# Products over eight neighbours in place, sums in halves, and one repeating load for each tile of neighbours

## The chip, the cores and the metric

One core of a Trainium2 chip runs the kernel in one launch. The metric is device time in microseconds, the median of three runs. The engines have a queue of instructions each and run side by side: PE (TensorE) multiplies matrices, PEld stands for its weight loads, DVE (VectorE) and ACT (ScalarE) work on rows of 128 partitions, POOL (GpSimd) helps, and SP (SyncE) issues transfers. SPq, DVEq and so on stand for an engine's queue.

## The reference, cut to what matters

The model is three residual blocks on `x` of shape (16, 64, 256). Inputs, weights and the two blocks that the change doesn't touch are left out.

```python
x = x + xattn(layernorm(x), ctx)      # quantised self and cross attention, ctx (16, 1601, 256)
x = x + attn(layernorm(x))            # below
x = x + ffn(layernorm(x))

def attn(x, ...):                     # NH = 16 heads, HD = 16, NB = 8 blocks, bt = 64 // 8 = 8 tokens
    h = rmsnorm(x, attn_norm_w)
    qkv = bitlinear(h, qkv_w).reshape(B, S, 3, NH, HD)
    ...
    q = apply_rope(q, cos, sin)
    k = apply_rope(k, cos, sin)
    qb, kb, vb = (blk(q), blk(k), blk(v))                       # (B, NB, NH, bt, HD)
    scores = jnp.einsum('bnhqd,bnhkd->bnhqk', qb, kb) * HD ** -0.5
    scores = jnp.where(causal, jnp.finfo(scores.dtype).min, scores)
    attn = jax.nn.softmax(scores, axis=-1)
    ctx = jnp.einsum('bnhqk,bnhkd->bnhqd', attn, vb)
    ...
    x1 = x + bitlinear(ctx, o_w)
    hn = rmsnorm(x1, ffn_norm_w)
    gate, val = jnp.split(hn @ ffn_up_w.T, 2, axis=-1)
    return x1 + bitlinear(jax.nn.silu(gate) * val, ffn_down_w)
```

Every token attends to the at most eight tokens of its own block: a row of queries meets eight rows of keys and eight rows of values, its neighbours. `bitlinear` quantises its input by rows (`act_quant`) and has ternary weights.

## The kernel before, in words

**Tiles and streams.** The 1024 rows of `x` are eight tiles of 128 rows, `NT = 8`, sixteen blocks of eight tokens in each. For every tile there are four units of the cross attention (two halves of the heads, two batch items), and a unit walks through the 1601 rows of `ctx` in chunks. A chunk loads context (`ctxT`, L608, and `ctxN`, L617), projects keys (`ps_k`, L624), copies them as 16-bit halves (`kh`, L651), stores these to DRAM (`kd`, L655), loads them back transposed (`kT`, L665, a transposing transfer), multiplies with the queries (`s`, L696), exponentiates on ACT (`P`, L706), keeps a running maximum on DVE (`M`, L715; maxima over the transposed `tr_m`, L721 and L723, then `tr_r`, L438), applies the maximum (`P`, L754 on DVE and L758 on ACT) and sums over the values (`acc`, L772). A unit ends in reciprocals and divisions (`rvx` and `pq`, L785 to L790), transposes (`tr_pc`, L799) and `po_x` (L863), whose result goes through `q_y` (L875) and a rounding to 8 bits into `cat` (L319) and the output projection (`po_p`, L332, weights in two halves `w_hi` and `wproj`, L309 and L310). The self attention (`ps_q`, `ps_kv`, L379, weights `wq` and `wkv`, loaded on L301) runs beside it.

**The stage of the change.** `last_parts(i)` (L1068) computes for tile i the block attention and the feed-forward part. It runs while the units of later tiles are at work; the last tile's has no units left beside it. Normalise and quantise (`act_quant`, whose transposes are `tr_aq`, L997), project to `qk` and `v3`, rotate, and then, for all tiles but the last:

- the rotated keys and the values go to DRAM (`kv`, L1127) in two halves of eight heads, 128 columns each;
- `near(kv, e, a)` (L1003) loads a half back so that each of the 128 rows holds all eight rows of its block, 8 x 128 numbers. Eight transfers do that: number k writes the k-th row of each of the sixteen blocks, 16 rows of 4 KB, 64 KB;
- `product` (L1010), for each half of the keys, multiplies with the row's queries into a new tile `prod` (L1013) and sums over the 16 features (L1014) into the scores `sc`;
- softmax over the eight neighbours (L1139 to L1150);
- `product` again, for each half of the values, multiplies with the scores and sums over the eight neighbours into `cx`;
- `act_quant` of `cx`, the transposes `tr_aq`, the output projection `po_o` (L1168), and the feed-forward part.

The values are loaded (L1138) after the scores' products have been written down. The last tile (7) doesn't use `near` and `product`: it selects neighbours by matmuls (`block_scores`, `block_values`), and its `block_values` sums in halves (L1061 to L1063).

**Buffers.** `near` and `prod` tiles come from the pool `wp`, ten buffers of 128 x 1024 numbers, which the weights (`wq`, `wkv`, `wqx`, `wproj`, `w_hi`, `sel` and others) use as well. A middle tile takes four buffers for `near` and four for `prod`.

**Order.** The streams are generators on a heap: each has a step and a rank, and what it yields, changed by a list of offsets by hand (`PACE`), is the step at which it goes on. This gives the order in which the program is written down. A scheduler then orders each engine's instructions by its own estimates, so the order on an engine can differ from the program's and can move with an edit. On the chip each queue runs in that order and nothing overtakes. SP issues nearly all transfers; eight semaphores for them are used in turn, and an issue waits for the one eight before it. In the last span, groups of the late feed-forward (`late_chunk`, matmuls `pgu_late`, L1255, four to a chunk) are put between the steps of the last tile to keep PE at work.

```python
def paced(name, gen):
    d = PACE.get(name, ())
    for k, w in enumerate(gen):
        yield max(w + (d[k] if k < len(d) else 0), 0.01)
```

Of the kernel before, what the change touches and what calls it, by code (L numbers as in the profile page):

```python
# [14 lines left out]
F32 = mybir.dt.float32  # L15
# [4 lines left out]
ALU = mybir.AluOpType  # L20
AX = mybir.AxisListType
PSUM = bass.MemoryType.PSUM

P = 128
# [49 lines left out]
def body(tc, ctx, a):  # L74
    nc = tc.nc
    V, A, PE, GP = nc.vector, nc.scalar, nc.tensor, nc.gpsimd
# [3 lines left out]
    wp = ctx.enter_context(tc.tile_pool(name="wp", bufs=10))  # L80
# [861 lines left out]
    def b1(name, dt=F32):  # L942
        return one.tile([P, 256 if dt == F32 else 512], dt, tag="b1", name=name, bufs=4)

    def b2(name):
        return one.tile([P, 512], F32, tag="b2", name=name, bufs=3)
# [56 lines left out]
    def near(kv, e, a):  # L1003
        t = wp.tile([P, 1024], F32, tag="w", name="near")
        src = kv[e, a].rearrange("(n j) c -> n (j c)", j=8)
        for k in range(8):
            nc.sync.dma_start(out=t.rearrange("(n t) x -> n t x", t=8)[:, k, :], in_=src)
        return t

    def product(out, x, y, order):  # L1010

        t = wp.tile([P, 1024], F32, tag="w", name="prod")
        V.tensor_tensor(t.rearrange("p (h j d) -> p h j d", h=8, j=8), x, y, ALU.mult)  # L1013
        V.reduce_sum(out, t.rearrange("p (h j d) -> p " + order, h=8, j=8), axis=AX.X)  # L1014

    def gathered(src, c):

# [8 lines left out]
    def block_scores(rotate, r1, r2, sc):  # L1026
        rotate(16, 32, V)
        V.tensor_tensor(r1[:, H : 2 * H], r1[:, H : 2 * H], r2[:, H : 2 * H], ALU.add)
        yield 1
        keys = [gathered(r1[:, H : 2 * H], c) for c in range(4)]  # L1030
        rotate(0, 16, V)
        V.tensor_tensor(r1[:, 0:H], r1[:, 0:H], r2[:, 0:H], ALU.add)
        yield 1
        for d in range(2):
            fill("sc%d" % d)
            t = wp.tile([P, 1024], F32, tag="w", name="prod").rearrange("p (j x) -> p j x", j=4)
            for e in range(2):
                V.tensor_tensor(
                    t[:, 2 * e : 2 * e + 2], keys[2 * d + e], r1[:, 0:H].unsqueeze(1).to_broadcast([P, 2, H]), ALU.mult
                )  # L1040
            V.reduce_sum(
                sc[:, :, 4 * d : 4 * d + 4].rearrange("p h j -> p j h"), t.rearrange("p j (h d) -> p j h d", h=16), axis=AX.X
            )
            yield 1

    def block_values(sc, v3, cx):
        ts = []
        for d in range(2):
            fill("av%d" % d)
            t = wp.tile([P, 1024], F32, tag="w", name="prod").rearrange("p (j x) -> p j x", j=4)  # L1050
            for e in range(2):
                c = 2 * d + e
                V.tensor_tensor(
                    t[:, 2 * e : 2 * e + 2].rearrange("p j (h d) -> p j h d", h=16),
                    gathered(v3, c).rearrange("p j (h d) -> p j h d", h=16),
                    sc[:, :, 2 * c : 2 * c + 2].rearrange("p h j -> p j h").unsqueeze(3).to_broadcast([P, 2, 16, 16]), ALU.mult,
                )
            ts.append(t.rearrange("p j x -> p (j x)"))
            yield 1
        x, y = ts  # L1060
        V.tensor_tensor(x, x, y, ALU.add)  # L1061
        V.tensor_tensor(x[:, 0:512], x[:, 0:512], x[:, 512:1024], ALU.add)
        V.tensor_tensor(cx, x[:, 0:H], x[:, H : 2 * H], ALU.add)  # L1063
        yield 1
# [3 lines left out]
    def last_parts(i, start):  # L1068
# [6 lines left out]
        h = b1("h")  # L1075
# [26 lines left out]
        r1, r2 = b2("r1"), b2("r2")  # L1102
        r24 = r2.rearrange("p (h e d) -> p h e d", h=32, e=2)

        def rotate(h0, h1, eng):
            n = h1 - h0
            eng.tensor_tensor(
                r1.rearrange("p (h d) -> p h d", h=32)[:, h0:h1], qk.rearrange("p (h d) -> p h d", h=32)[:, h0:h1],
                rope[:, 0:16].unsqueeze(1).to_broadcast([P, n, 16]), ALU.mult,
            )  # L1110
            for e in range(2):
                V.tensor_tensor(
                    r24[:, h0:h1, e, :], q4[:, h0:h1, 1 - e, :],
                    rope[:, 16 + 8 * e : 24 + 8 * e].unsqueeze(1).to_broadcast([P, n, 8]), ALU.mult,
                )

        sc = one.tile([P, 16, 8], F32, tag="sc3", name="sc3")
        if last:
            yield from block_scores(rotate, r1, r2, sc)
        else:  # L1120
            rotate(0, 32, GP)
            yield 1
            V.tensor_tensor(r1, r1, r2, ALU.add)
            yield 1
            kv = dram.tile([2, 2, P, P], F32, tag="kv3", name="kv3")
            for e, t in ((0, r1[:, H : 2 * H]), (1, v3)):
                nc.sync.dma_start(out=kv[e].rearrange("a p c -> p a c"), in_=t.rearrange("p (a c) -> p a c", a=2))  # L1127
            yield 1
            near_k = [near(kv, 0, a) for a in range(2)]
            yield 2  # L1130
            for a in range(2):
                product(
                    sc[:, 8 * a : 8 * a + 8, :],
                    r1[:, a * P : (a + 1) * P].rearrange("p (h d) -> p h d", h=8).unsqueeze(2).to_broadcast([P, 8, 8, 16]),
                    near_k[a].rearrange("p (j h d) -> p h j d", j=8, h=8), "h j d",
                )
                yield 1
            near_v = [near(kv, 1, a) for a in range(2)]  # L1138
        V.tensor_tensor(sc, sc, cmask.unsqueeze(1).to_broadcast([P, 16, 8]), ALU.add)  # L1139
# [12 lines left out]
        cx = one.tile([P, H], F32, tag="cx3", name="cx3")  # L1152
        if last:
            yield from block_values(sc, v3, cx)
        else:
            for a in range(2):
                product(
                    cx[:, a * P : (a + 1) * P].rearrange("p (h d) -> p h d", h=8),
                    sc[:, 8 * a : 8 * a + 8, :].unsqueeze(3).to_broadcast([P, 8, 8, 16]),
                    near_v[a].rearrange("p (j h d) -> p h j d", j=8, h=8), "h d j",  # L1160
                )
                yield 1
        to = ternary_piece(1536, 512).rearrange("p (k o) -> p k o", k=2)
        yield 1
# [179 lines left out]
    for i in range(NT):  # L1344
        base = 52 * i
        for hh in range(2):
            for bb in range(2):
                unit(i, hh, bb, base + 26 * hh + 13 * bb)
            spawn(base + 26 * hh + 13 + 34 - 2 + (2, 1)[hh], 6.5, paced("pair", pair_out(i, hh, 4 if i < NT - 1 or hh == 0 else None)))
        ln0, sa0, qx0 = SCHEDULE[i] if i in SCHEDULE else (  # L1350
            base - 22, [base + o for o in (-15, 0, 8, 21)], [base + o for o in (-16, -7, 15, 18)]
        )
        spawn(ln0, 1.0, paced("ln" if i else "ln_first", ln_tile(i)))
        for p in range(4):
            spawn(sa0[p] - 2, 5.0, paced("sa", self_attention(i, p)))
            spawn(qx0[p] - 2, 3.0, paced("qx", queries(i, p)))
        l0 = base + {NT - 3: 95, NT - 2: 88, NT - 1: 82}.get(i, 90)
        spawn(l0, 4.5, paced("last" if i < NT - 1 else "last_tile", last_parts(i, l0)))
    spawn(-4.5, 1, bias_rows())
    spawn(60, 5.7, ternary())  # L1360
    order = [(kind, p) for p in range(4) for kind in ("wq", "wkv", "wqx", "wproj")]
# [76 lines left out]
```

## Time and profile before

| what | value |
|---|---|
| median of 3 runs | 2376.91 us (2375.15, 2376.91, 2381.84) |
| the profiled execution | 2381.09 us |
| its span, first to last instruction | 2379.3 us |
| granted TensorE clock, mean of the span | 0.996 |
| bytes moved, mean rate | 482.82 MB, 203 GB/s |
| costliest groups on PE | `acc` L772 799.8 us, `ps_k` L624 757.7 us, `s` L696 411.9 us |

The table's durations are sums over all instructions of a line. The profile is of one execution; times within it count from its first instruction. A line of the timeline gives start and duration in us, engine, line, operation, the tiles written and read, their shapes and how many instructions stand together; in square brackets is how long the engine was idle before and what ended the wait. A line that groups instructions by form gives their number, the least, median and largest duration in ns, and the first and last start in us.

### The profile page before, as it was taken

The page shows a single profiled execution, that of the slowest core. Times are in us where ns is not written, and L with a number is a line of the kernel's source. Part 1 is how long each engine was busy: PE and PEld are TensorE (multiplying, and loading weights), DVE is VectorE, ACT ScalarE, POOL GpSimd, SP SyncE. Part 2 cuts the span into 40 slices and gives each one's busy share as a digit, 9 for nine tenths or more (in the row PEclk, how much of TensorE's full clock was granted, in tenths as well). Part 3 has the DMA queues.
Part 4 walks back from the last instruction along what each step waited for, and adds up shares of the span by engine and source line. Part 5 has one row for each costly group of instructions (what it writes and reads, how often), then busy time and mean ns, then how long its engine had stood idle before and what let it go on. Part 6 is the DMA issues. An engine that isn't in the chain of part 4 may idle for free.

```text
span 2379.3 us, 40465 instructions
## 1 busy us (share of the span) xinstructions
PE 2318.1 (97%) x12501; PEld 1766.1 (74%) x12509; DVE 1844.9 (78%) x4786; ACT 1670.7 (70%) x3729; POOL 746.6 (31%) x967
## 2 busy tenths in 40 slices
PE   7999999999999999999999999999999999999997
PEld 4677777777787777777778777777777777677876
DVE  6777768878878788787887879777888777876766
ACT  6767767776776777767776777777677777676631
POOL 3323223332332333332332323334333333232200
PEclk9999999999999999999999999999999999999999
DMA  8989878777977698776887769777698776965332
GB/s 271 281 234 252 231 177 240 206 186 187 269 206 195 173 224 246 195 202 176 234 230 196 202 183 248 217 196 190 179 258 212 188 184 173 276 174 140 116 98 72
DMA packets 682094, 482.82 MB, mean 203 GB/s; under 512 B 463932, under 2 KB 591896, under 8 KB 681880
## 3 DMA queue, kind: packets, MB, share of 16 engines
q1 hardware_dynamic: 681592, 480.08, 75.4%
q8 instruction: 100, 1.64, 0.3%
q14 instruction: 114, 0.93, 0.1%
q10 hardware_dynamic: 288, 0.17, 0.0%
HBM read 268.93 MB, written 112.85 MB: 160 GB/s over the span
## 4 chain that ended last, share of the span: by engine, by line
PE 75%; DVE 9%; DMA 5%; ACT 4%; issue 3%; POOL 3%; SPq 0%; ACTq 0%; DVEq 0%; POOLq 0%
PE acc L772 23%; PE ps_k L624 22%; PE s L696 13%; PE po_x L863 2%; PE po_p L332 2%; DMA kd<-kh 2%; PE ps_q L379 2%; ACT P L706 1%; DMA kT<-kd 1%; PE tr_pc L799 1%; POOL rsx L568 1%; DVE P L754 1%; PE sc L490 1%; POOL rs L226 1%; PE po_f L1274 1%
## 5 line engine op out<-in xcount | busy, mean ns | idle before, releaser
L772 PEld LDWEIGHTS acc<-ctxN,P 128*128 128x128 f32 (+1 forms) x4160 | 713.3, 191 | 212.6 <-issue 134.9
L772 PE MATMUL acc<-ctxN,P 128*128 128x257 f32 (+5 forms) x4160 | 799.8, 338 | 5.4 <-DMA ctxN<-in_ctx_n 3.3
L624 PE MATMUL ps_k<-wkx,ctxT 128*128 128x512 f32 x1600 | 757.7, 595 | 11.6 <-DVE wkx L1331 9.4
L567 POOL TENSOR_SCALAR vx<-ss 128x4 f32<-128x4 f32 (+1 forms) x402 | 162.2, 403 | 1215.3 <-DVE ss L564 803.9
L706 ACT ACTIVATE P<-s,rsx 128x128 f32<-128x128 f32 x1536 | 441.0, 374 | 142.4 <-PE s L696 131.4
L568 POOL TENSOR_TENSOR rsx<-vx,nhalf 128x4 f32<-128x4 f32 (+1 forms) x402 | 442.6, 1101 | 32.7
L624 PEld LDWEIGHTS ps_k<-wkx,ctxT 128*128 128x128 f32 x1600 | 277.3, 191 | 208.9 <-issue 188.9
L696 PE MATMUL s<-qx,kT 128*128 128x128 f32 x3072 | 411.9, 277 | 8.2 <-ACT qn L389 4.4
L696 PEld LDWEIGHTS s<-qx,kT 128*128 128x128 f32 x3072 | 377.2, 192 | 24.8 <-ACT qn L389 6.2
L715 DVE TENSOR_TENSOR M<-P,M 128x512 f32<-128x512 f32 (+1 forms) x384 | 263.0, 685 | 167.4 <-ACT P L706 146.0
L758 ACT ACTIVATE P<-P 128x512 f32<-128x512 f32 (+1 forms) x416 | 266.6, 642 | 154.9 <-DVE P L754 153.6
L651 ACT COPY kh<-ps_k 128x1024 uint16<-128x1024 uint16 x360 | 366.8, 1019 | 8.9 <-DMA kd<-kh 8.9
L559 ACT ACTIVATE sq<-ps_k 128x512 f32<-128x512 f32 (+1 forms) x402 | 243.4, 605 | 156.2 <-PE ps_k L624 128.0
L564 DVE TENSOR_REDUCE ss<-sq 128x4 f32<-128x512 f32 (+1 forms) x402 | 272.0, 677 | 18.9 <-ACT sq L559 18.5
L754 DVE TENSOR_TENSOR P<-P,mx 128x512 f32<-128x512 f32 (+1 forms) x416 | 283.2, 681 | 0.0
L226 POOL TENSOR_TENSOR rs<-ve,nhalf 128x4 f32<-128x4 f32 (+2 forms) x112 | 114.9, 1027 | 241.4 <-DVE ve L223 218.6
L232 DVE TENSOR_SCALAR qn<-qn,mv,rs 128x128 f32<-128x128 f32 x256 | 77.2, 340 | 47.8 <-POOL rs L226 47.1
L310 DVE TENSOR_TENSOR wproj<-wproj,w_hi 128x1024 fp32r<-128x1024 f32 x60 | 73.0, 1218 | 12.9 <-ACT w_hi L309 12.2
L309 ACT CAST w_hi<-wproj 128x1024 fp32r<-128x1024 f32 x60 | 63.4, 1058 | 26.8 <-DMA wproj<-wproj 26.0
L219 DVE BATCH_NORM_STATS2 st<-qn 128x6 f32<-128x128 f32 x256 | 64.5, 270 | 18.8 <-ACT qn L389 18.8
L332 PE MATMUL po_p<-wproj,cat 128*128 128x256 f32 x272 | 67.1, 293 | 0.0
L332 PE MATMUL po_p<-w_hi,cat 128*128 128x256 f32 x240 | 65.9, 308 | 0.9 <-ACT qk L1091 0.9
(254 smaller groups left out, 2763.7 us busy)
## 6 DMA issues: line engine op xcount, KB each, us to landing
kd<-kh SPq DMA_DIRECT2D x375, 256.0 KB
ctxT<-in_ctx SPq DMA_DIRECT2D x192, 256.0 KB
ctxN<-in_ctx_n SPq DMA_DIRECT2D x384, 128.0 KB
wproj<-wproj SPq DMA_DIRECT2D x68, 512.0 KB
wq<-wq SPq DMA_DIRECT2D x32, 512.0 KB
wkv<-wkv SPq DMA_DIRECT2D x32, 512.0 KB
wqx<-wqx SPq DMA_DIRECT2D x32, 512.0 KB
near<-kv SPq DMA_DIRECT2D x224, 64.0 KB
```

What stands on the lines that cost most here:

```text
L332: PE.matmul(po[:, 0:H], lhsT=cat[:, h, :], rhs=w[:, h * H : (h + 1) * H], start=h + e == 0, stop=h == 3 and e == len(ws) - 1,)
L559: A.activation(sq[:n], ps[:n], AF.Square)
L564: ordered("dve", V.reduce_sum(ss[:n], sq[:n].rearrange("p (g d) -> p g d", g=4), axis=AX.X))
L568: ordered("pool", GP.tensor_tensor(rs[:n], ve[:n], nhalf[:n, 0:4], ALU.pow))
L624: PE.matmul(ps[:n, :], lhsT=st["cxT"][c // 2][:, k, o : o + n], rhs=wkx[:, k, 512 * hh : 512 * (hh + 1)], start=k == 0, stop=k == 1,)
L651: A.copy(t, src.bitcast(U16).rearrange("p (c e) -> p e c", e=2))
L696: PE.matmul(ps[:n, g * P : (g + 1) * P], lhsT=kT[:, g, 0:n], rhs=qxs[i, hh][:, bb, 2 * g : 2 * g + 2, :].rearrange("p h s -> p (h s)"), st ...
L706: A.activation(pc[:, g * P : (g + 1) * P], ps[:, g * P : (g + 1) * P], AF.Copy, scale=rs[:, g : g + 1])
L715: ordered("dve", V.tensor_tensor(st["M"][:n], pc[:n], st["M"][:n], ALU.max))
L754: ordered("dve", V.tensor_tensor(pc[:n], pc[:n], st["mx"][:n].rearrange("p g q -> p (g q)"), ALU.add))
L758: A.activation(pc[:n], pc[:n], AF.Exp)
L772: m = PE.matmul(ps, lhsT=pc[:n, g * P : (g + 1) * P], rhs=cx[:n, o : o + w], start=g < 3 and c == 0, stop=c == NC - 1, skip_group_check=g ...
```

## The change

Two things are done in the middle tiles 0 to 6, and the last tile's code stays. `near` issues one transfer in place of eight: its source names the block's 4 KB row eight times (a repeat with a step of zero as the second dimension, behind the sixteen blocks), its destination is the whole tile of 128 rows. `product` is replaced by two functions that need no tile of their own. `near_scores` multiplies into the `near` tile itself, laid out neighbour by neighbour, and sums over the features. `near_values` multiplies into the `near` tile, and sums over the neighbours by adding the upper half to the lower: 512 numbers, 256, and 128 into `cx`.

```diff
     def near(kv, e, a):
         t = wp.tile([P, 1024], F32, tag="w", name="near")
         src = kv[e, a].rearrange("(n j) c -> n (j c)", j=8)
-        for k in range(8):
-            nc.sync.dma_start(out=t.rearrange("(n t) x -> n t x", t=8)[:, k, :], in_=src)
+        nc.sync.dma_start(out=t, in_=src.unsqueeze(1).to_broadcast([16, 8, 1024]))
         return t

-    def product(out, x, y, order):
-
-        t = wp.tile([P, 1024], F32, tag="w", name="prod")
-        V.tensor_tensor(t.rearrange("p (h j d) -> p h j d", h=8, j=8), x, y, ALU.mult)
-        V.reduce_sum(out, t.rearrange("p (h j d) -> p " + order, h=8, j=8), axis=AX.X)
+    def near_scores(out, x, y):
+
+        y = y.rearrange("p (j x) -> p j x", j=8)
+        V.tensor_tensor(y, x.unsqueeze(1).to_broadcast([P, 8, P]), y, ALU.mult)
+        V.reduce_sum(out, y.rearrange("p j (h d) -> p h j d", h=8), axis=AX.X)
+
+    def near_values(out, x, y):
+
+        y4 = y.rearrange("p (j h d) -> p j h d", j=8, h=8)
+        V.tensor_tensor(y4, x.rearrange("p h j -> p j h").unsqueeze(3).to_broadcast([P, 8, 8, 16]), y4, ALU.mult)
+        for n in (512, 256):
+            V.tensor_tensor(y[:, 0:n], y[:, 0:n], y[:, n : 2 * n], ALU.add)
+        V.tensor_tensor(out, y[:, 0:P], y[:, P : 2 * P], ALU.add)
...
             near_k = [near(kv, 0, a) for a in range(2)]
             yield 2
             for a in range(2):
-                product(
-                    sc[:, 8 * a : 8 * a + 8, :],
-                    r1[:, a * P : (a + 1) * P].rearrange("p (h d) -> p h d", h=8).unsqueeze(2).to_broadcast([P, 8, 8, 16]),
-                    near_k[a].rearrange("p (j h d) -> p h j d", j=8, h=8), "h j d",
-                )
+                near_scores(sc[:, 8 * a : 8 * a + 8, :], r1[:, a * P : (a + 1) * P], near_k[a])
                 yield 1
             near_v = [near(kv, 1, a) for a in range(2)]
...
             for a in range(2):
-                product(
-                    cx[:, a * P : (a + 1) * P].rearrange("p (h d) -> p h d", h=8),
-                    sc[:, 8 * a : 8 * a + 8, :].unsqueeze(3).to_broadcast([P, 8, 8, 16]),
-                    near_v[a].rearrange("p (j h d) -> p h j d", j=8, h=8), "h d j",
-                )
+                near_values(cx[:, a * P : (a + 1) * P], sc[:, 8 * a : 8 * a + 8, :], near_v[a])
                 yield 1
```

The steps that the generator yields, and the offsets in `PACE`, are the same in both.

## The prediction

> **What bounds the kernel now.** I began with the totals and the chain of work that ended last.
>
> ```profile
> span 2379.3 us, 40465 instructions
> PE 2318.1 (97%) x12501; PEld 1766.1 (74%) x12509; DVE 1844.9 (78%) x4786; ACT 1670.7 (70%) x3729; POOL 746.6 (31%) x967
> PE 75%; DVE 9%; DMA 5%; ACT 4%; issue 3%; POOL 3%; SPq 0%; ACTq 0%; DVEq 0%; POOLq 0%
> near<-kv SPq DMA_DIRECT2D x224, 64.0 KB
> ```
>
> TensorE works 97% of the span: it idles 2379.3 − 2318.1 = 61 us. Nothing the change touches makes a matmul shorter, so it can only fill or open idle time of PE. Adding the pauses between matmuls longer than 0.4 us in the trace gives 48.1 us: 10.3 before 150 us, 23.1 between 150 and 2250, 14.7 after 2250. So VectorE's saved microseconds are worth nothing as such; I look for the pauses beside `near` and its products. Two kinds stand out.
>
> The first is in the timeline of the first tile's values (start us, duration, engine, line, operation), with the chain of waits there.
>
> ```profile
> 564.85 10.59 SPq L1007 DMA_DIRECT2D near<-kv  x16
> 578.99 5.89 DMA kd<-kh
> 584.24 1.54 PE L772 MATMUL acc<-ctxN,P 128*128 128x257 f32 x6 [1.36 <-DMA ctxN<-in_ctx_n]
> 584.89 1.01 ACT L651 COPY kh<-ps_k 128x1024 uint16<-128x1024 uint16 x1 [0.99 <-DMA kd<-kh]
> 586.04 1.13 PE L696 MATMUL s<-qx,kT 128*128 128x128 f32 x8 [0.26 <-ACT kh L651]
> ```
>
> Sixteen issues hold SP's queue for 10.6 us; key stores, key transposes and context loads stand behind them, the next key store lands 5.89 us after its issue, and PE stands 1.36 + 0.26 = 1.62 us. The bursts of the next tiles (851.6, 1138.8, 1424.1, 1701.9, 2007.9) are followed by PE pauses of 1.32, 1.09, 1.02, 0.66 and 1.45.
>
> The second is after tile 6's values, where the last unit's matmuls have run out (the last line is a window's totals: its ends, its length, PE, PEld, VectorE, ScalarE and GpSimd busy, granted clock, DMA share, GB/s).
>
> ```profile
> 2267.09 0.39 PE L997 MATMUL tr_aq<-identb,aq_q 128*128 128x128 bf16 x2 [4.05 <-DVE aq_q L989]
> 2268.02 0.61 PE L1168 MATMUL po_o<-tern_w,aq_t 128*128 128x256 bf16 x2 [0.54 <-DVE aq_t L999]
> 2268.42 3.62 PE L863 MATMUL po_x<-pc,wvx 128*128 128x256 f32 x8
> 2266.00:2273.00 7.00, 5.37 (x15) 4.14 (x16) 5.29 (x20) 2.53 (x5) 0.93 (x1) 0.52 0.40 141
> ```
>
> PE waits 4.05 + 0.54 us for `act_quant` of `cx`, and then the granted clock is 0.52 with PE busy 5.37 us: eight `po_x` matmuls take 3.62 us there and 1.89 at 544.2. Half of the 5.37 is lost, 2.7 us. The same follows the pause of 5.30 us at 2341.4, but not the short ones.
>
> **The change part by part.**
>
> ```profile
> L1007 SPq DMA_DIRECT2D near<-kv  x224: 471/587/1386, 520.4 to 2244.8; - x112
> L1013 DVE TENSOR_TENSOR prod<-sc,near x14: 1215/1217/1220, 578.1 to 2258.4; 128x1024 f32<-128x1024 f32 x14
> L1014 DVE TENSOR_REDUCE sc<-prod x14: 1207/1210/1214, 544.8 to 2229.7; 128x64 f32<-128x1024 f32 x14
> L1014 DVE TENSOR_REDUCE cx<-prod x14: 1854/1892/1907, 580.4 to 2260.1; 128x128 f32<-128x1024 f32 x14
> L1062 DVE TENSOR_TENSOR prod<-prod x1: 692/692/692, 2343.4 to 2343.4; 128x512 f32<-128x512 f32 x1
> L1063 DVE TENSOR_TENSOR cx<-prod x1: 427/427/427, 2344.1 to 2344.1; 128x256 f32<-128x256 f32 x1
> ```
>
> *Transfers.* 32 issues a tile become 4: 28 × 0.59 = 16.4 us of SP's queue a tile, 115 us in seven tiles. The values' burst of 10.6 us becomes two issues of about 0.5 us, so stores and transposes behind it go out some 9 us earlier. The same 512 KB a half still moves: 128 packets of 4 KB at 0.2 us over 16 engines, 1.6 us, two halves 3.2 us instead of 10.6 in which the trickle left room for others. A store right behind may thus find 3.2 us of queue, still less than the hold removed. I take the five pauses of tiles 0 to 4 as gone: 1.62 + 1.32 + 1.09 + 1.02 + 0.66 = **5.7 us** (bounds: none, if the 3.2 us do the same; 11.5, half of the middle's 23.1, if the freed queue heals others too).
>
> *Products.* The multiplications keep their size and 1.22 us; that they now write over their operand should change nothing, as the in-place sum of the same size on line 310 takes 1.22 too (bounds 1.21 and 1.23). The scores' reduction still has the 16 features innermost: 1.21 us. The values' reduction of 1.89 us becomes sums over 512, 256 and 128: 0.69 + 0.43 + 0.28 (rows of 128x128, 281 to 291 ns) = 1.40, −0.49 each, 14 × 0.49 = 6.9 us of VectorE; starts of consecutive instructions lie closer than durations (0.60 for a 0.69), so up to 14 × 0.66 = 9.2. All of it lies beside PE, except in tile 6's chain, where it is counted below. Four fewer tiles a tile from the ten buffers of `wp` (near and prod: 8 to 4) let weight loads start earlier; I count no gain, and that more can stand behind one another is in the first rival.
>
> *Order.* The static order of instructions moves with it. In the changed kernel the loads of the keys' halves are issued where the first of the sixteen was (520.4 in tile 0), and the first scores product stands in VectorE's queue right after the copy of `pT`, a queue in which nothing overtakes:
>
> ```profile
> 520.40 0.58 SPq L1007 DMA_DIRECT2D near<-kv  x1
> 522.06 0.42 DVE L514 COPY pT<-tr_p 128x256 f32<-128x256 f32 x1
> 524.17 0.69 DVE L715 TENSOR_TENSOR M<-P,M 128x512 f32<-128x512 f32 x1 [1.69 <-ACT P L706]
> 525.97 0.66 DVE L785 RECIPROCAL rvx<-acc 128x1 f32<-128x1 f32 x4
> 530.57 0.60 PE L799 MATMUL tr_pc<-ident,pq 128*128 128x128 f32 x4
> ```
>
> VectorE gets there at 522.5. A 512 KB load beside it in time (`wq`, 550.84) lands 3.76 us after issue; over all `wq` loads the landings take 3.21 at least, 4.86 in the median, 6.93 at the 90th percentile. At 3.76 the product waits until 524.2, 1.7 us, inside the 1.69 us that VectorE idles there. Behind it stand maxima M (0.6 to the next), softmax P (0.6), a `wproj` half of 1.14 that moves ahead, reciprocals 0.55, a sum 0.6, three divisions 0.92, with the product's 1.2 in front: `pq` is ready 5.6 us after the landing, and PE asks for it at 530.57. So a landing up to 4.4 us after the issue costs nothing; the median, 4.86, costs 0.4; 6.93 costs 2.4. What covers it is VectorE's idle time and the queue of matmuls ahead of `tr_pc`. In tile 5 both scores products and one reduction (3.6 us) stand ahead of `cat`, which ends at 1967.5 now: 1971.1, and near 1972.5 with a landing wait a little under tile 0's; PE's `po_p` asks for it at 1970.1 now, about 1970.9 in the new order: 1.6 us, which cancels that tile's 1.45. In tile 6 the scores product stands ahead of a maximum for `tr_r` and makes it 1.0 us late. I take **−2.5** for the waits of tiles 0 to 4 (bounds 0 and 5 × 2.4 = 12), **0** for tile 5, **−1.0** for tile 6.
>
> *The end.* In the changed order tile 6's value chain stands about five steps of the unit earlier: its `tr_aq` comes after 3 of the last unit's `acc` groups, not 23. The pauses 4.05 + 0.54 and the 2.7 of clock go: 7.3. But one late gate chunk, four matmuls, 1.7 us with their pauses, that filled PE during the last tile's softmax, moves out of that shadow. Net **+5.6** (bounds: −1.7, if the chain is late all the same; 7.3).
>
> The Trainium skill, "TensorE: Matmul & The Clock Gate" (Part 1: The HAM clock gate), has the clock halved after an idle window of about 3.4 us. The pauses of 4.05 and 5.30 and the half clock behind them agree; by the rule a pause cut to 3 us would already save the 2.7, by the trace alone only its removal.
>
> The skill's "DMA: Bandwidth & Descriptors" (Rules for kernel authors) speaks against a repeating transfer whose outermost dimension is small: a leading repeat of c confines it to c engines. Here the 16 blocks are outermost and the 8 repeats second, so by the rule all 16 engines work; were it eight, 1.6 us of moving would be 3.2, and the median landing 6.5.
>
> **Sum.** 5.7 − 2.5 + 0 − 1.0 + 5.6 = 7.8 us off the profiled execution's 2381.09: 2373.3. That execution lies 4.2 above the median of the runs shown, 2376.91; carried over to it the forecast is **2369.1**.
>
> **The rivals.** About 7.1 us (0.3%) is what a measurement of this kernel can tell from no change.
>
> *First, slower: the landing decides.* The scores product waits in VectorE's queue in front of maxima and softmax that PE needs. It decides from a landing 4.4 us after issue; at 6.93 each of seven tiles loses 2.5 (6.9 − 4.4): 2369.1 − 2.5 + 7 × 2.5 = 2384; at 7.5, between this and the longest `wq` landing of 8.52, 2369.1 − 2.5 + 7 × 3.1 = **2388**, my price for it; it is even with the kernel before at 5.9. For it: the `wq` loads' spread and the two loads of a pair in one queue. Against: the one near it in time took 3.76.
>
> *Second, no change: the end stays as it is.* Something else keeps tile 6's chain late, the clock halves all the same and the chunk costs its 1.7: 2369.1 + 5.6 + 1.7 = 2376.4. For it: its scores still wait for loads issued after 2196. Against: the moved order.
>
> *Third, faster still: the queue decides.* 115 us fewer of SP's queue also shorten the later pauses (787, 1747, 2027 to 2031): 11.5 in place of 5.7, and no new waits: 2369.1 − 5.8 − 2.5 = 2361. Against: most of these pauses name no DMA.
>
> **How the numbers follow.** Forecast 0.41, of which 0.27 faster and 0.14 within 0.3% (its own range 2363 to 2375, the bounds of the waits and of the end in part); first rival 0.24 (0.17 slower, 0.07 same); second 0.22 (0.02 faster, 0.16 same, 0.04 slower); third 0.13 (0.12 and 0.01). Faster 0.41, same 0.38, slower 0.21. The range runs from the third rival's 2361 to 2385, between the first one's 2384 and 2388, with about a tenth outside on each side.
>
> **What would show it.** The repeating load at 0.4 to 0.6 us an issue, landing in 3.5 to 4.9; no PE pause over 0.5 us within 25 us behind the value loads; PE pause at tile 6's `tr_aq` under 1 us and clock 1.0 behind it; idle of VectorE before the scores product about 1.7. Wrong if PE waits for `tr_pc` or `tr_m` beside the loads by more than 1 us a tile, or if the half clock stays.

## The result and the profile after

The changed kernel is slower: 2402.43 us, median of 4 runs (2401.43 to 2409.27), beside 2379.38 (2375.15 to 2385.46) for the kernel before in its 4 runs. The ratio is 1.0101 with a 95% interval of 1.0085 to 1.0116, some 23 us. The profiled execution took 2409.27 us, 28.2 more than that of the kernel before.

The totals of the changed kernel's page, the chain that ended last by engine, and the transfers:

```profile
span 2407.5 us, 40230 instructions
PE 2325.8 (97%) x12509; PEld 1771.6 (74%) x12509; DVE 1833.2 (76%) x4814; ACT 1666.6 (69%) x3729; POOL 766.2 (32%) x967
PE 70%; DVE 12%; DMA 6%; issue 5%; POOL 4%; ACT 2%; SPq 0%; POOLq 0%; ACTq 0%; DVEq 0%
near<-kv SPq DMA_DIRECT2D x28, 512.0 KB
```

The edit did what it says: 28 issues in place of 224, and VectorE works 11.7 us less. But the idle time of PE went from 61.2 to 81.7 us (span less busy), and PE's busy time from 2318.1 to 2325.8 for the same matmuls, which is the granted clock (0.996 before, 0.992 after). On the chain VectorE, DMA, GpSimd and bare issue gained what PE and ScalarE lost. The timeline of tile 0's keys shows the first new pause (start us, duration, engine, line, operation):

```profile
523.51 0.64 SPq L1006 DMA_DIRECT2D near<-kv  x1
527.96 1.23 DVE L1012 TENSOR_TENSOR near<-r,near 128x1024 f32<-128x1024 f32 x1 [2.37 <-DMA near<-kv]
533.21 0.74 DVE L529 TENSOR_TENSOR q_y<-po_s,rsc 128x256 f32<-128x256 f32 x2
533.67 0.50 PE L379 MATMUL ps_q<-w_hi,xq 128*128 128x512 f32 x1 [1.61 <-DVE q_y L529]
```

The load lands 4.4 us after its issue. VectorE stands 2.37 us at the scores product, and `q_y`, which stands behind it, lets PE go on with `ps_q` 1.61 us late. In tiles 1 to 4 this pause is 2.08, 2.79, 3.37 and 2.31. In all five tiles VectorE reaches the product 2.1 us after the issue; the loads land after 4.42, 4.90, 5.61, 6.17 and 5.14 us, and each pause is its landing less 2.8 us. The kernel before took this `ps_q` without a pause, 2.2 us ahead of `tr_pc` (530.57):

```profile
528.39 0.79 PE L379 MATMUL ps_q<-w_hi,xq 128*128 128x512 f32 x1
```

The second new pause comes some 50 us later:

```profile
574.63 0.57 SPq L301 DMA_DIRECT2D wq<-wq  x1
579.54 1.04 ACT L309 CAST w_hi<-wq 128x1024 fp32r<-128x1024 f32 x1 [4.00 <-DMA wq<-wq]
580.62 1.22 DVE L310 TENSOR_TENSOR wq<-wq,w_hi 128x1024 fp32r<-128x1024 f32 x1 [2.07 <-ACT w_hi L309]
583.31 0.63 PE L721 MATMUL tr_m<-ident,M 128*128 128x128 f32 x4 [3.20 <-DVE M L727]
```

Here no `near` tile is waited for at all. A weight load has moved earlier in SP's queue (596.15 before), its cast on ScalarE has moved closer still, and ScalarE stands 4.00 us at it; the maximum behind it makes PE wait 3.20 us. In tiles 1 to 4: 0.87, 2.05, 3.08 and 2.14. In tiles 5 and 6 the scores products stand in front of `cat` and of `red`:

```profile
2005.06 0.55 PE L332 MATMUL po_p<-w_hi,cat 128*128 128x256 f32 x1 [4.84 <-DVE cat L319]
2238.54 0.27 PE L438 MATMUL tr_r<-ident,red 128*4 128x128 f32 x1 [2.72 <-DVE red L723]
```

The waits of VectorE (engine, line and releaser: us in total, times, longest) give one sum for it, which no row of the kernel before has:

```profile
DVE near L1012 <- DMA near<-kv: 25.2, 8, 4.6
```

The pauses cost more than their length. Windows behind the pause of tile 1 (bounds, length, then PE, PEld, VectorE, ScalarE and GpSimd busy, granted clock, DMA share, GB/s):

```profile
820.00:823.00 3.00, 0.92 (x3) 0.26 (x2) 3.00 (x12) 1.98 (x7) 1.26 (x2) 1.00 0.96 287
823.80:827.20 3.40, 3.40 (x10) 2.07 (x9) 3.40 (x13) 3.03 (x5) 0.00 (x0) 0.50 1.10 228
```

A pause of 2.08 us is followed by 3.4 us at half clock. From 500 to 2300 us the changed kernel spends 30.7 us at half clock in eight such spells (one of 6.8 us), the kernel before 6.8 us in one.

Where the time went, by the last `ps_k` matmul of all units as a mark: it starts at 2240.0 before and 2277.9 after, 37.9 us later. From there to the end it is 139.3 us before and 129.6 after, 9.7 less. PE's pauses over 0.4 us between 500 and 2260 us grew from 15.0 to 40.2, by 25.2; that leaves some 13 of the 37.9 for the clock, about what PE's busy time differs from that of a run without spells in the middle (2325.8 and 2312.1). The end was won as foreseen. The first line is the kernel before, the second the changed one:

```profile
2250.00:2300.00 50.00, 44.67 (x242) 37.38 (x241) 34.73 (x77) 18.32 (x32) 1.48 (x2) 0.93 0.46 145
2250.00:2300.00 50.00, 49.99 (x295) 41.40 (x294) 36.16 (x76) 32.81 (x78) 11.41 (x14) 1.00 0.29 94
```

PE is full and at full clock where it was busy for 44.67 of 50 us at 0.93; tile 6's `tr_aq` (2293.5 now) waits for nothing.

### The profile page after: what moved, and what is told of

It reads as the page before. It is cut to its first block, busy times and chain, and to the rows that moved or that the text cites. A ratio compares the mean times of both kernels' runs of the same rounds, so it can differ in the third digit from the quotient of the medians.

```text
span 2407.5 us, 40230 instructions
## 1 busy us (share of the span) xinstructions
PE 2325.8 (97%) x12509; PEld 1771.6 (74%) x12509; DVE 1833.2 (76%) x4814; ACT 1666.6 (69%) x3729; POOL 766.2 (32%) x967
## 4 chain that ended last, share of the span: by engine, by line
PE 70%; DVE 12%; DMA 6%; issue 5%; POOL 4%; ACT 2%; SPq 0%; POOLq 0%; ACTq 0%; DVEq 0%
PE acc L772 22%; PE ps_k L624 21%; PE s L696 11%; PE po_p L332 2%; PE po_x L863 2%; PE ps_q L379 2%; POOL rs L226 1%; DVE P L754 1%; POOL rsx L568 1%; DMA wq<-wq 1%; DMA near<-kv 1%; DVE M L715 1%; PE tr_pc L799 1%; DVE qn L232 1%; PE sc L490 1%
## 5 line engine op out<-in xcount | busy, mean ns | idle before, releaser
L567 POOL TENSOR_SCALAR vx<-ss 128x4 f32<-128x4 f32 (+1 forms) x402 | 176.1, 438 | 1242.6 <-DVE ss L564 933.3
```

## The experiments

My theory after the result (A): the loss is one of order. An engine's queue is fixed ahead of time by the scheduler's estimates, and the edit moves consumers of 512 KB loads to places where the load hasn't landed, with other work behind them. The rivals: (B) the 512 KB repeating transfers crowd the DMA queue, wherever they are waited for; (C) the new products cost.

All ratios below are against runs of the kernel before, measured beside them on the same chip, with 95% intervals.

**The change taken apart.** The transfer alone, with the old `product`:

```diff
-        for k in range(8):
-            nc.sync.dma_start(out=t.rearrange("(n t) x -> n t x", t=8)[:, k, :], in_=src)
+        nc.sync.dma_start(out=t, in_=src.unsqueeze(1).to_broadcast([16, 8, 1024]))
```

> The one repeating transfer for each near tile, with the old products (a prod tile of their own, reduction over the neighbours). Its static order has the first scores product behind q_y and the divisions, not ahead of them, but the weight loads and their casts on ScalarE close together as in the changed kernel. Theory A (order: an engine stands at the head of its queue for a load that the new order brings too close): PE's pauses before ps_q of 1.6 to 3.4 us in tiles 0 to 4 go (sum 12.2), those before tr_m stay in the main (sum 11.3): 10 to 14 us above the kernel before. Theory B (the 512 KB repeating transfers crowd the DMA queue, wherever the waits stand): the same 23 us above as the changed kernel. Theory C (the new products cost): no slower than before.

Measured: 2389.60 us, ratio 1.0044 (1.0026 to 1.0063), 10.9 above. No pause before `ps_q` in any tile; 13.7 us of pauses before `tr_r`, the next step after `tr_m`, in tiles 0 to 4. As theory A has it: in tile 0 ScalarE stands 4.24 us at the cast of `wq`, and `red` stands behind that cast's second half on VectorE.

The products alone (the other hunks of the change, with the eight transfers kept):

> The new products in place and the sums in halves, with eight transfers for each near tile. Its static order is that of the kernel before nearly everywhere. Theory A: within 5 us of the kernel before. Theory B: the same, since the transfers are the old ones. Theory C: most of the 23 us.

Measured: 2383.76 us, 1.0021 (1.0012 to 1.0031), 5.0 above, at the edge of what A and B allow. The 4 us pause before tile 6's `tr_aq` and the half clock behind it are still there, so the shorter chain of VectorE didn't cure them. One new pause is larger than the whole difference: 4.50 us before `ps_q` at 2029.4, with 3.4 us of half clock, where the values products stand in VectorE's queue ahead of the second half of `wq`. No load is waited for there, so an order can cost without a late landing. Theory C is out as the main cause; but 10.9 + 5.0 don't make 23 either, so the parts act on one another.

One transfer for the values, eight for the keys, new products; and the reverse, with `e == 0` in its first line:

```diff
+        if e == 1:
             nc.sync.dma_start(out=t, in_=src.unsqueeze(1).to_broadcast([16, 8, 1024]))
+        else:
+            for k in range(8):
+                nc.sync.dma_start(out=t.rearrange("(n t) x -> n t x", t=8)[:, k, :], in_=src)
```

> The changed kernel with eight transfers for the keys' tiles and one for the values' tiles. The static order around the scores product and the casts is the old one. Theory A: no slower than before, and up to 6 us faster, as the burst of sixteen issues is gone and the kd stores behind it land 2 us earlier; no pauses before ps_q or tr_m. Theory B: about half of the 23 us, 10 to 13 above, since half of the repeating transfers are left.

> The changed kernel with one transfer for the keys' tiles and eight for the values' tiles. Theory A: the scores product stands ahead of the divisions and PE pauses before ps_q as in the changed kernel (sum 12 us in tiles 0 to 4), but the second cast of wq stands later in ScalarE's queue, so the pauses before tr_m go: 8 to 16 above the kernel before. Theory B: about half of the 23 us in any places.

Measured: values by one 2364.73 us, 0.9941 (0.9920 to 0.9963), 14 us faster than the kernel before. Keys by one 2380.49 us, 1.0014 (1.0001 to 1.0026). The first speaks against B outright: half of the repeating transfers are there and the time falls. Its gain is more than I expected, since tile 6's end is cured as well. In the second the pauses are the ones that I named, at the same places:

```profile
525.75 1.23 DVE L1016 TENSOR_TENSOR near<-r,near 128x1024 f32<-128x1024 f32 x1 [2.57 <-DMA near<-kv]
531.47 0.50 PE L379 MATMUL ps_q<-w_hi,xq 128*128 128x512 f32 x1 [1.80 <-DVE q_y L529]
```

They sum to 11.0 us in tiles 0 to 4 (12.2 in the changed kernel), and those before `tr_m` are gone. But the total lay under my 8 to 16, because the end was won here too, and because the pauses before `acc` and `s` behind the value loads are gone as well: the sixteen issues are still there, but no more than seven stand in a row.

The sums in halves and the one transfer, but each product written to a `prod` tile of its own:

```diff
+        t = wp.tile([P, 1024], F32, tag="w", name="prod").rearrange("p (j x) -> p j x", j=8)
-        V.tensor_tensor(y, x.unsqueeze(1).to_broadcast([P, 8, P]), y, ALU.mult)
-        V.reduce_sum(out, y.rearrange("p j (h d) -> p h j d", h=8), axis=AX.X)
+        V.tensor_tensor(t, x.unsqueeze(1).to_broadcast([P, 8, P]), y.rearrange("p (j x) -> p j x", j=8), ALU.mult)
+        V.reduce_sum(out, t.rearrange("p j (h d) -> p h j d", h=8), axis=AX.X)
...
```

> The changed kernel with sums in halves, but each product written to a prod tile of its own from the pool of ten buffers, as before. The scores product then waits in the scheduler's eyes for a free buffer and stands behind q_y and the divisions. If the place of the scores product follows from the buffer that the in-place product no longer needs, this runs as the kernel with the one transfer and the old products, 2390 (within 4), and without pauses before ps_q. If the new order comes from the products themselves, it stays near 2402.

Measured: 2402.64 us, 1.0086 (1.0063 to 1.0109). A half miss: the places came out as in the first case, the time as in the second. The pauses before `ps_q` are gone, as the place of the scores product does follow from the buffer. But the casts' pauses grew to 22.5 us in their place, and the time stayed. The timeline of its tile 1:

```profile
862.78 0.35 SPq L301 DMA_DIRECT2D wq<-wq  x1
868.53 1.04 ACT L309 CAST w_hi<-wq 128x1024 fp32r<-128x1024 f32 x1 [3.83 <-DMA wq<-wq]
871.59 0.37 PE L438 MATMUL tr_r<-ident,red 128*4 128x128 f32 x1 [5.49 <-DVE red L723]
```

The load lands 5.73 us after its issue, and ScalarE, then VectorE, then PE stand one behind the other. With the old reduction (the run of the transfer alone) this pause was 3.02 us: the same transfers in another order, and another pause.

**The order alone.** The kernel has a helper that draws an edge between two instructions for the scheduler, `behind` (one engine's order; the chip waits for nothing more). With it the order can be changed and all transfers and products kept. First the scores product:

```diff
-        V.tensor_tensor(y, x.unsqueeze(1).to_broadcast([P, 8, P]), y, ALU.mult)
+        behind(V.tensor_tensor(y, x.unsqueeze(1).to_broadcast([P, 8, P]), y, ALU.mult), mark["dve"])
```

> The changed kernel, all transfers and products as they are, with one edge for the scheduler alone (no wait on the chip): each scores product stands behind the last running maximum or shift that the program has written down before it. In VectorE's order the first one of tile 0 moves from ahead of the divisions to behind q_y of po_x. Theory A (order): the pauses before ps_q (12.2 us in tiles 0 to 4) and before po_p in tile 5 (4.8) go, with some 5 us of half clock behind them; those before tr_m stay, as the casts on ScalarE keep their place: 2380 to 2390. Theory B (the transfers themselves): within 5 us of the changed kernel's 2402.

then the casts:

```diff
-            A.activation(pc[:n], pc[:n], AF.Exp)
+            mark["exp"] = A.activation(pc[:n], pc[:n], AF.Exp)
...
-        A.copy(hi, ws.bitcast(F32))
+        cast = A.copy(hi, ws.bitcast(F32))
+        if "exp" in mark:
+            behind(cast, mark["exp"])
```

> The changed kernel with an edge for the scheduler on ScalarE instead: each cast w_hi stands behind the last exponential written down before it. The second cast of wq moves back by about eight groups of instructions. The scores product moves too, behind the variance for qn. Theory A: the pauses before tr_m (11.3 us in tiles 0 to 4, and their half clock) go; the scores product's wait stays in some form: 2380 to 2392. Theory B: within 5 us of 2402.

then both:

> Both edges. Theory A: no pauses beside the near loads over 1 us, one transfer for keys as well as values, and the time of the kernel with one transfer for the values alone, 2365, or a few us less: 2358 to 2368. Theory B: within 5 us of 2402.

Measured: 2390.41, 1.0039 (1.0025 to 1.0053); 2390.80, 1.0028 (1.0009 to 1.0046); both 2373.13, 0.9963 (0.9948 to 0.9979). The kernel before had a median of 2383.22 beside them. Each edge alone takes over half of the loss, and both together more than all of it. B is refuted: not a byte of the transfers differs. In the run with the edge on the product the pauses before `ps_q` went and those behind the casts stayed, as expected, but these grew to 17.1 us before `tr_r` in tiles 0 to 4 and 6.1 before `tr_m` in tile 5; its time is just above my range. In the run with the edge on the casts I had expected the pauses before `tr_m` to go; 22.6 us of pauses stayed before `tr_m` and `tr_r` in tiles 0 to 4, while those before `ps_q` went, so that one was right in its time and wrong in its places (its profile is of its fastest execution, 2380.84 us). The run with both edges missed its range of 2358 to 2368, and has five pauses of 2.1 to 3.7 us before `tr_r` where I had expected none over 1 us. They show in its timeline:

```profile
561.55 1.23 DVE L1020 TENSOR_TENSOR near<-sc,near 128x1024 f32<-128x1024 f32 x1 [1.22 <-DMA near<-kv]
575.56 0.27 PE L440 MATMUL tr_r<-ident,red 128*4 128x128 f32 x1 [2.40 <-DVE red L725]
```

and in its chain of waits (start us, us, what):

```profile
555.23 6.23 DMA near<-kv
```

It is a third place of the same kind: the values product stands in front of the normalisation of `qn`, `kn` and of `red`, while its load takes 6.23 us. Only 1.22 of the 2.40 us are this wait (0.9 to 3.8 us in tiles 0 to 4), and not the 6 to 7 us that I name below; the rest is the products' own work ahead of `red`. So I held it too, two steps later in the program:

```diff
+            yield 2
             for a in range(2):
                 near_values(cx[:, a * P : (a + 1) * P], sc[:, 8 * a : 8 * a + 8, :], near_v[a])
...
-        V.tensor_tensor(y4, x.rearrange("p h j -> p j h").unsqueeze(3).to_broadcast([P, 8, 8, 16]), y4, ALU.mult)
+        behind(V.tensor_tensor(y4, x.rearrange("p h j -> p j h").unsqueeze(3).to_broadcast([P, 8, 8, 16]), y4, ALU.mult), mark["dve"])
```

> The changed kernel with three edges for the scheduler: scores product and casts as in the run with both edges, and the values product, two steps later, behind the last maximum or shift written down before it, which puts it behind the maximum red that PE waits for. In the run with both edges the pauses left beside the loads (2.1 to 3.7 us before tr_r, sum 13 in tiles 0 to 4, with four spells of half clock) stood where the values product waited 6 to 7 us ahead of red for its load. If that is all that is left: ratio 0.988 to 0.993, pauses before tr_r under 1 us. If the load's waits only move on to what stands behind it now: ratio near 0.996 as with both edges.

Measured: 2355.77 us, 0.9906 (0.9892 to 0.9921). It beats both kernels: 21.6 us under the kernel before, measured beside it. Its windows in tiles 0 and 1, columns as above:

```profile
550.00:600.00 50.00, 49.90 (x278) 38.65 (x277) 44.38 (x106) 39.06 (x85) 20.57 (x23) 1.00 0.91 228
800.00:850.00 50.00, 49.88 (x274) 38.74 (x273) 43.97 (x107) 38.99 (x84) 17.65 (x22) 1.00 1.03 238
```

and its timeline at the place of the last wait:

```profile
574.50 0.69 DVE L725 TENSOR_REDUCE red<-tr_m 128x4 f32<-128x512 f32 x1 [2.20 <-PE tr_m L723]
575.34 0.27 PE L440 MATMUL tr_r<-ident,red 128*4 128x128 f32 x1
576.04 1.22 DVE L1020 TENSOR_TENSOR near<-sc,near 128x1024 f32<-128x1024 f32 x1
```

`red` now stands ahead of the values product, which no longer waits, and PE has no pause over 0.4 us between 400 and 1936 us. Yet the `near` loads land later here than in the changed kernel (median 6.7 us after issue, 5.9 there): what a load takes didn't matter once nothing urgent stood behind its consumer. What it has lost again is the end: from the last `ps_k` on it takes 136.7 us, where the changed kernel took 129.6, with 6.8 us at half clock behind tile 6's `tr_aq`.

**What is then worth what.** The transfer for the values alone in the kernel before, old products, no edges:

> The kernel before with one repeating transfer for the values' tiles alone; keys and products as before. It asks which half of the change brought the 14 us that the kernel with new products and one transfer for the values gained. If it is the transfer (the burst of sixteen issues gone, 5.7 us of pauses; tile 6's chain earlier, up to 7): 2364 to 2370, ratio near 0.995. If the new products are needed (tile 6's shorter chain of VectorE, 2 x 0.7 us, is what brings tr_aq ahead of the end of the units): ratio 0.997 to 1.000, with the 4 us pause before tr_aq and the half clock behind it still there.

Measured: 2378.04 us, 0.9999 (0.9987 to 1.0010). Neither of my two pictures: the pause before tile 6's `tr_aq` is gone and the bursts' pauses too, but there are 7.8 us of pauses before `tr_r` in tiles 0 to 4, where the two values products stand ahead of `red` without waiting for a load, and 7.8 before `ps_g` (3.8 in the kernel before), whose cause I didn't follow. The run with the new products (0.9941) has none of the first and 4.4 us of the second.

The kernel before with the three edges, and the transfer alone with the three edges:

> The kernel before, with its eight transfers and its old products, and the three edges and the two steps of the fastest run. It asks whether that run's gain comes from the order alone. The burst of sixteen issues for the values is still there, and PE's pauses behind it with it (5.7 us in tiles 0 to 4). If the order alone brings the gain: ratio 0.989 to 0.993. If the change is needed for it: 0.996 to 1.003, with the pauses at acc or s behind each burst.

> The one repeating transfer with the old products (prod tiles, reduction over the neighbours) and the same edges. Without edges this was 1.0044 of the kernel before. If the waits at the head of a queue were all of its loss: 0.990 to 0.995, at most 3 us behind the kernel with new products and edges (14 x 0.66 us of VectorE, mostly hidden). If 512 KB transfers or the prod buffers cost by themselves: 1.000 or more.

Measured: the kernel before with edges 2394.57, 1.0074 (1.0059 to 1.0089); the transfer alone with edges 2355.28, 0.9913 (0.9897 to 0.9929). So these edges alone are no gain, they are a loss for eight transfers, outside what I had expected of them. Its timeline in tile 0 says why, and its chain of waits there:

```profile
565.71 9.96 SPq L1009 DMA_DIRECT2D near<-kv  x16
584.39 2.91 PE L774 MATMUL acc<-ctxN,P 128*128 128x257 f32 x6 [2.29 <-DMA ctxN<-in_ctx_n]
```

```profile
578.67 5.58 DMA ctxN<-in_ctx_n
```

A context load right behind the burst lands 5.58 us after its issue, and PE stands for it. With the rest of the order tight, the burst is the bound: 17.2 us of pauses before `s` and `acc` in tiles 0 to 4. Whether the eight transfers would do as well at this order with their issues spread out, as in the run with one transfer for the keys, wasn't tried. With the three edges the one transfer is worth the whole difference from 1.0074 to 0.9913, while in-place products and sums in halves are worth nothing that the runs can tell (0.9906 and 0.9913, intervals over one another).

## Why the prediction was wrong

I forecast 2369.1, a range of 2361 to 2385, and slower with 0.21. Point by point:

- *The five pauses behind the value loads, 5.7 us:* right. PE's pauses before `acc` and `s` behind them are gone in the changed kernel. That sixteen issues in a row are their cause, the run of the kernel before with edges shows, and the run with one transfer for the keys, where the issues are spread and the pauses gone. What went is the hold of SP's queue and not the landing: the first key store behind tile 0's value loads still lands 5.80 us after its issue, 5.89 behind the burst.
- *The end, +5.6:* right in its mechanism, too small: 9.7 us from the last `ps_k` to the end. `tr_aq` no longer waits, and the clock is full. By the profile the surplus came from the clock: from that mark on the half-clock time fell from 17.4 to 3.4 us, 7.0 at half speed, where I had 2.7. Part of it lies behind the last tile's pause, which stayed 5.3 us long; I hadn't foreseen that and count it as luck.
- *Products beside PE, worth nothing as such:* right, as the two held runs show.
- *The waits of tiles 0 to 4, −2.5:* this is the step that failed. I followed the scores product to `pq` and `tr_pc`, and set the harmless landing at 4.4 us. PE's next claim was not `tr_pc` but `ps_q`, which needs `q_y` behind the same product: a landing of 4.42 cost 1.61 us. The harmless landing was thus 2.8 us in tiles 0 to 4, not 4.4. The kernel before shows that claim already, ahead of `tr_pc` (528.39 and 530.57). And the landings weren't the 3.76 of the one row near in time, but 4.42 at least and 5.9 in the median of all 28 (the median of `wq` is 4.4 in the trace of the kernel before, not 4.86). Together 12.2 us where I had 2.5.
- *The order elsewhere:* the larger omission. I saw that four fewer buffers let weights load earlier and that this "can stand behind one another", and counted nothing. The second cast of `wq` on ScalarE, placed right behind its load, cost 11.3 us in tiles 0 to 4. I had compared the new order where the edited lines stand, and not along ScalarE's queue.
- *Tile 5, 0, and tile 6, −1.0:* right places, too small. The product in front of `cat` cost 4.84 us, where I had 1.6; a 2.66 us pause before `tr_r` came on top; tile 6 lost 2.72.
- *The clock:* I let only pauses over 4 us halve it. The trace of the kernel before says otherwise: at 2361.8 it has 3.4 us of half clock behind pauses of 1.13 and 0.52 us. Of the new pauses of 2 to 3.4 us in tiles 0 to 4 six of eight did so, and two in tile 5, in all some 13 us.

One sum of the prediction is mislabelled: 48.1 us is the total of all pauses between matmuls. Those over 0.4 us sum to 40.2 (9.0, 17.1 and 14.1), which makes the upper bound for the value loads 8.6, not 11.5, and the third rival's time 2364; the forecast doesn't rest on it.

The first rival (the landing decides) was the right mechanism, with 0.24 and a price of 2388. It had one of three places in it, and no clock. The experiments settle that the loss goes with the order: the same transfers and arithmetic lose 1% in one order and gain 1% in another. What isn't shown is why the scheduler's estimates lead to just these places; that they take a 512 KB load for shorter than it is, I only infer from where engines stood: in tiles 0 to 4 VectorE and ScalarE reached these consumers 0.4 to 2.1 us after issues whose loads landed 4.4 to 6.2 us after them.

## What to carry to other kernels

When a scheduler writes the queues, an edit to the loads or the buffers can move their consumers forward, and an engine that works in order then stands for the landing with everything behind it. Compare the static order on every engine, weight casts far from the edit included, and price each consumer at the landings of loads of its size in that stage. If a saving disappears, try the same instructions with the consumers held by order edges before giving it up: here the same change went from 1.0101 to 0.9906. The edges have to fit the kernel: on the kernel before the same three cost 0.7%.

## What the runs showed of the hardware

The granted clock falls to half after pauses of PE well under 3.4 us. Over the fourteen profiles of this study, from 150 us on, it fell after 4 of 22 pauses of 1.5 to 2 us, 18 of 32 of 2 to 3 us, 7 of 10 of 3 to 3.5 us, and all 28 longer ones, in spells of 3.4 or 6.8 us. Eleven more spells stand behind two or more pauses under 1.5 us each, a few us apart, so the length of one pause isn't all that counts. The Trainium skill, "TensorE: Matmul & The Clock Gate" (Part 1: The HAM clock gate), speaks of an idle window of about 3.4 us; here half of that could do. As an estimate from the spells, a pause of 2 to 3 us is to be priced at up to 1.7 us more than its length, or 3.4 where the spell is of 6.8 us (3 of the 18).

The repeating 512 KB load took 4.3 us at the least and 5.6 to 7.3 in the median of a kernel from issue to landing, later than weight loads of the same size (4.5 to 5.1), though it reads only 64 KB of different data; in the changed kernel the second of a pair took up to 8.3, and a weight load right behind one 8.7. Nothing shows it on fewer DMA engines than they use: each of the 28 loads completes in sixteen steps of its semaphore, as theirs do, and where one is alone with its 4 KB packets (8 of the 28 in the changed kernel), about 11 of these are under way at a time, as there. But such a packet takes 0.22 us in the median, 0.16 there. That it always lands later than a plain load I haven't tried by itself.
